# Attention kernel, two score phases: the 128-column round of heads 2, 3 ahead of the 64-column round

## The chip, the cores and the metric

The kernel runs on one core of a Trainium2 chip. The metric is device time in microseconds (us) for one launch, the median of several runs. TensorE (PE) does the matrix products, ScalarE (ACT) the exponentials and copies out of PSUM, VectorE (DVE) the additions, GpSimd (POOL) the causal masks, and SyncE (SP) issues most of the DMAs.

## The reference, cut to what matters

```python
B, C, H, W = x.shape                       # 32, 256, 32, 32; S = H * W = 1024
xf = group_norm(x).reshape(B, C, S)        # 32 groups
q = einsum('oc,bcs->bos', q_w, xf) + q_b   # 256 channels = 8 heads of 32
k, v = split(einsum('oc,bcs->bos', kv_w, xf) + kv_b)
scores = einsum('bhqd,bhkd->bhqk', q, k) / sqrt(32)
scores = where(mask == 0, -10000, scores)  # a key counts only if it is before the query
attn = where(mask == 0, 0, softmax(scores))
out = x + einsum('bhqk,bhkd->bhqd', attn, v)
```

Everything is float32. The trace shows each float32 matrix product of the program as two MATMUL rows, called its first and second pass below.

## The kernel before

The batch of 32 images is walked one after the other. The eight heads are two groups of four (`g` = 0, 1); head `j` of a group has rows 32j to 32j+31 of `q` and `k`, and so its own 32 rows of the PE array. Scores are made transposed: keys on partitions, queries along the free axis. Each group has six visits (`VISITS`), so an image has twelve, `v` = 0 to 11 (`v` = 6g + i). One visit consists of a score phase (`scores`, all of its products go through line 329), some projections (`pp`, `ppv`, line 173) and the products with the values of the visit before (`acc`, line 451). The whole order is written out by hand and kept as written; PE gets its instructions in this order.

A score phase fills three PSUM tiles of two banks. `pairs[0]` holds the long product of heads 0, 1, `pairs[1]` that of heads 2, 3, and `pairs[2]` (`short`) the short products of all four heads. In visits with a diagonal (`PAIRS`, i = 0, 1, 3, 4), `pair` builds the short product out of two rounds for each head: a 128-column round and a 64-column round. Each round is 2 heads x 2 halves of 64 keys, four products, which use four separate pieces of 32 rows x 64 columns of the array. So heads 2, 3 use one half of the array's rows and heads 0, 1 the other half, and products of the one half run beside products of the other.

The order in a phase: short rounds of heads 2, 3 (`first`); long product of heads 0, 1 (`begin`); long product of heads 2, 3; a wait of PE on the semaphore `bank_free`; short rounds of heads 0, 1. The wait is there because heads 0 and 2 share a bank of `short`, as do heads 1 and 3: the last product of each head and half of `first` (`made[-1]`) counts `bank_free` up. After the phase ACT takes the exponentials: of `pairs[0]`, of `pairs[1]`, and of `short`.

Some phases put a piece of the long product between the two rounds of heads 2, 3 (`between` in `scores_of`). In visit i = 0 this is a separate product of 128 columns. In the visits `v` = 3 and 4 (`SPLIT`; not in the last image) `part_of` makes two pieces of the long product of heads 0, 1: columns 0 to 127 and columns 128 to 511. `order` gives the sequence of the rounds: -1 turns it around, so that the 64-column round comes first. The visits `v` = 1, 7, 9 and 10 are not split: both rounds of heads 2, 3 follow each other, 128 columns first, and then comes the 512-column product of heads 0, 1.

Of the kernel before, what the change touches and what calls it, by code (L numbers as in the profile page):

```python
# [32 lines left out]
def tile_norm_attention_residual(  # L33
# [69 lines left out]
    def unshifted():  # L103
# [230 lines left out]
        def scores_of(b, g, bank_of, heads, entries, between=lambda: None, order=slice(None)):  # L334

            done = {}
            for _, _, halves in entries:
                for k, n in enumerate(list(range(max(map(len, halves))))[order]):
                    if k:
                        between()  # L340
                    for j in heads:
                        for c, ops in enumerate(halves):
                            if n < len(ops):
                                done.setdefault((j, c), []).append(score(b, g, bank_of(j), j, ops[n]))
            return done

        def part_of(b, g, bank, entry, of):

            at, _, halves = entry
            for j in (0, 1):  # L350
                for ((c, kb, first, _, cols),) in halves:
                    score(b, g, bank[:, j, :], j, (
                        c, kb, first + of.start, of.stop - of.start, slice(cols.start + of.start, cols.start + of.stop)
                    ))

        def mask(b, g, raw, j):


            hf, place = j // 2, (2 * j % 4) * P
            if ("e", b, g, "D", hf) not in live:  # L360
                live["e", b, g, "D", hf] = epool.tile(
                    [P, 4, HALF], F32, tag=("e0", "e")[hf], bufs=4, name=f"diagonal_{b}_{g}_{hf}"
                )
            square = live["e", b, g, "D", hf]
            for s in range(2):
                nc.gpsimd.affine_select(  # L366
                    out=square[:, :, place + s * P : place + (s + 1) * P],
                    in_=raw[:, :, (1 - s) * KEYS : (3 - s) * KEYS],
                    pattern=[[0, 4], [(1, -1)[s], P]], compare_op=ALU.is_gt, fill=0.0, base=0,
                    channel_multiplier=(-1, 1)[s],  # L370
                )
            if j == 0:
                nc.gpsimd.memset(square[0:1, :, 0:1], 1.0)

        def scores(b, v):


            g, i = divmod(v, len(VISITS))
            longs, shorts = VISITS[i]
            name = f"{b}_{g}_{i}"  # L380
            e = epool.tile([P, 4, HALF], F32, tag="e0" if i == TOTAL else "e", bufs=4, name=f"e_{name}")
            eh = epool.tile([P, 4, HALFBANK], F32, tag="eh", bufs=3, name=f"eh_{name}")
            pairs = [ps_s.tile([P, 2, HALF], F32, tag="sT", name=f"sT_{name}_{a}") for a in range(3)]
            short = pairs[2].rearrange("p bank (n q) -> p bank n q", n=2)
            short_of = lambda heads, *how: scores_of(
                b, g, lambda j: short[:, j % 2, j // 2, :], heads, shorts, *how
            )
            long_of = lambda heads, n: scores_of(b, g, lambda j: pairs[j // 2][:, j % 2, :], heads, longs[n : n + 1])
            rest = [lambda: long_of((2, 3), 1)] if len(longs) > 1 else []
            begin = [lambda n=n: long_of((0, 1), n) for n in range(len(longs) - 1, -1, -1)]  # L390
            if b < B - 1 and v in SPLIT:
                begin = [lambda n=n: part_of(b, g, pairs[0], longs[0], n) for n in (slice(0, P), slice(P, HALF))]
            if i in PAIRS and len(begin) > 1:
                first = short_of((2, 3), begin.pop(0), slice(None, None, -1))
            else:
                first = short_of((2, 3))
            for f in begin:
                f()
            long_of((2, 3), 0)

            ends = [made[-1] for made in first.values()]
            first = [ins for made in first.values() for ins in made]
            for ins in ends:
                ins.then_inc(bank_free, 1)
            for ins in first:
                tc.no_tile_sem_insts.add(ins.ins.name)
            live["free"] = live.get("free", 0) + len(ends)
            wait = nc.tensor.wait_ge(bank_free, live["free"])
            for ins in first:
                tc.declare_no_dep(wait.ins, ins.ins, reason="the semaphore orders them")  # L410
            made = short_of((0, 1), *rest if i in PAIRS else ())
            if i not in PAIRS:
                for f in rest:
                    f()
            for made in made.values():
                for lo in made:
                    for ins in first:
                        tc.declare_no_dep(lo.ins, ins.ins, reason="the semaphore orders them")
            wide, narrow = (max(at + width for at, width, _ in entries) for entries in (longs, shorts))
            for a in range(3):  # L420
                if a == 2:
                    exp = nc.scalar.activation(  # L422
                        eh.rearrange("p (n bank) q -> p bank n q", n=2)[:, :, :, :narrow], short[:, :, :, :narrow], AF.Exp
                    )
                else:
                    nc.scalar.activation(e[:, 2 * a : 2 * a + 2, :wide], pairs[a][:, :, :wide], AF.Exp)  # L426

            for ins in first:
                tc.add_to_no_dep_group(f"first_{name}", ins.ins)
                tc.add_to_no_dep_group("first", ins.ins)  # L430
            tc.declare_no_dep(exp.ins, group=f"first_{name}", reason="through the last two products")
            tc.declare_fence(exp.ins, group=f"first_{name}")
            live["e", b, g, "L", i], live["e", b, g, "H", i] = e, eh
            if i in PAIRS:
                mask(b, g, eh, PAIRS[i])
# [255 lines left out]
        with tc.manual_schedule(engines={ENG.PE, ENG.Activation, ENG.DVE, ENG.Pool, ENG.SP}):  # L691
# [47 lines left out]
            for b in range(B):  # L739
                first, last = b * N, b == B - 1  # L740
# [44 lines left out]
            for i in range(B * N + 1):  # L785
                if i < B * N:
                    scores(*divmod(i, N))
                for f in at.pop(i, ()):
                    f()
                b, v = divmod(i - 1, N)  # L790
                if i == B * N:

                    sums(3, SUMMED[v], False)
                if i:
                    for _ in range(EVEN.count((i - 1) % N) if i < B * N - N else 0):
                        nc.tensor.wait_ge(bank_free, live["free"])
                    values(b, v)
                    if b < B - 1 or v not in SUMMED or v == 1:
                        add_keys(b, v)
                if i in (B * N - 2, B * N - 1):  # L800

                    sums(3, SUMMED[v])
                for f in after.pop(i, ()):
                    f()
# [175 lines left out]
```

## Time and profile before

| | before |
|---|---|
| runs, median (lowest to highest) | 1791.58 us (1791.32 to 1792.56), 3 runs |
| profiled execution, span from first to last instruction | 1791.2 us |
| PE busy | 1782.1 us (99%) |
| DVE busy | 1669.4 us (93%) |
| ACT busy | 1441.4 us (80%) |
| POOL busy | 897.9 us (50%) |
| mean granted PE clock | 0.999 |
| one score phase `v` = 3, to the start of the next work on PE | 1.39 us |

The profiled execution is one run more, beside the three timed ones; its page gives the span and no further time. It is 0.4 us under the median and 0.1 us under the lowest run. Of the span, 31% of the chain of work that ended last is in the score products of line 329, all phases together. In the profile's rows `sT` stands for any of the three PSUM tiles of scores, and a form such as "32*64 32x128" is a product with 32 rows and 64 columns of weights and 128 moving columns. The end of a MATMUL row is modelled; its start is recorded.

### The profile page before, as it was taken

How to read it: one execution, taken by the hardware profiler on the slowest of the kernel's cores; microseconds unless marked ns; L12 is line 12 of the kernel's file. 1: busy time of each engine (PE TensorE's matmuls, PEld its weight loads, DVE VectorE, ACT ScalarE, POOL GpSimd, SP SyncE). 2: the span in 40 equal slices, each digit the busy share in tenths (PEclk: the TensorE clock that was granted, in tenths of full speed). 3: DMA queues.
4: the chain of work that ended last, by engine and by line, in shares of the span. 5: the costliest groups of instructions: out<-in, count | busy, mean ns of one | idle time of the engine just before them, and what ended most of it. 6: DMA issues, size and time to landing. Idle time of an engine off the chain costs nothing.

```text
span 1791.2 us, 81784 instructions
## 1 busy us (share of the span) xinstructions
PE 1782.1 (99%) x37036; PEld 936.1 (52%) x37036; DVE 1669.4 (93%) x1796; ACT 1441.4 (80%) x1928; POOL 897.9 (50%) x935
## 2 busy tenths in 40 slices
PE   9999999999999999999999999999999999999998
PEld 5555555555555555555555555555555555555554
DVE  4689999999999999999999999999999999999998
ACT  6888878888778788788887888877888878888785
POOL 2355554554555555545555555454455554554542
PEclk9999999999999999999999999999999999999999
DMA  2567766767677676676776676767766766777663
GB/s 72 105 117 142 137 133 135 148 138 147 128 142 138 137 141 138 132 144 142 142 138 134 137 142 138 150 129 140 139 145 131 141 136 135 149 138 141 133 109 98
DMA packets 92771, 240.21 MB, mean 134 GB/s; under 512 B 26272, under 2 KB 27792, under 8 KB 76544
## 3 DMA queue, kind: packets, MB, share of 16 engines
q0 software_dynamic: 17360, 100.58, 40.1%
q1 hardware_dynamic: 74912, 134.28, 25.9%
q8 instruction: 290, 4.75, 1.1%
q14 instruction: 65, 0.53, 0.1%
q10 hardware_dynamic: 144, 0.07, 0.0%
HBM read 69.90 MB, written 34.95 MB: 59 GB/s over the span
## 4 chain that ended last, share of the span: by engine, by line
PE 99%; DVE 0%; ACT 0%; issue 0%; POOL 0%; POOLq 0%
PE sT L329 31%; PE acc L451 28%; PE pp L173 27%; PE ppv L173 13%; PE pd L503 1%; PE busy L159 0%; PE wt L152 0%; ACT e L426 0%; DVE rb_last L576 0%; DVE rb_last L563 0%; DVE turned L560 0%; DVE acc L573 0%; DVE inv_last L562 0%; POOL ident masks.py:199 0%; PE pv L173 0%
## 5 line engine op out<-in xcount | busy, mean ns | idle before, releaser
L426 ACT ACTIVATE e<-sT 128x1024 f32<-128x1024 f32 x768 | 744.3, 1022 | 301.5 <-PE sT L329 298.8
L366 POOL TENSOR_SCALAR_AFFINE_SELECT diagonal<-eh 128x512 f32<-128x512 f32 x512 | 563.3, 1122 | 625.4 <-ACT eh L422 624.7
L469 DVE TENSOR_TENSOR e<-e,e 128x1024 f32<-128x1024 f32 x314 | 578.0, 1841 | 23.0 <-ACT v L293 3.5
L329 PE MATMUL sT<-q,k 32*64 32x64 f32 (+1 forms) x18928 | 577.9, 367 | 0.1
L329 PEld LDWEIGHTS sT<-q,k 32*64 32x64 f32 x18928 | 397.0, 131 | 203.8 <-PE sT L329 67.4
L173 PE MATMUL pp<-xn,wT 128*32 128x512 f32 x4096 | 492.3, 598 | 0.0
L451 PE MATMUL acc<-e,v 128*32 128x512 f32 (+3 forms) x4608 | 401.0, 450 | 0.0
L422 ACT ACTIVATE eh<-sT 128x768 f32<-128x768 f32 (+1 forms) x384 | 341.6, 890 | 0.0
L451 PEld LDWEIGHTS acc<-e,v 128*32 128x32 f32 x4608 | 149.2, 110 | 261.5 <-issue 239.0
L173 PE MATMUL ppv<-wT,xn 128*32 128x256 f32 x4096 | 247.5, 382 | 0.0
L469 DVE TENSOR_TENSOR diagonal<-diagonal,e 128x1536 f32<-128x1536 f32 x126 | 194.5, 1544 | 16.1 <-PE acc L451 6.5
L173 PEld LDWEIGHTS pp<-xn,wT 128*32 128x32 f32 x4096 | 107.0, 109 | 195.8 <-issue 163.7
L469 DVE TENSOR_TENSOR e<-e,eh 128x1024 f32<-128x1024 f32 x126 | 177.6, 1410 | 6.5
L451 PEld LDWEIGHTS acc<-diagonal,v 128*32 128x32 f32 x4096 | 120.9, 110 | 88.1 <-issue 68.2
L173 PEld LDWEIGHTS ppv<-wT,xn 128*32 128x32 f32 x4096 | 120.2, 109 | 80.0 <-issue 7.0
L469 DVE TENSOR_TENSOR e<-e,diagonal 128x2048 f32<-128x2048 f32 x63 | 144.0, 2285 | 18.9 <-POOL diagonal L366 18.7
L451 PE MATMUL acc<-diagonal,v 128*32 128x128 f32 x4096 | 158.9, 273 | 0.0
L205 POOL DMA_INDIRECT eight<-each,group_of x31 | 42.9, 1383 | 193.4 <-DMA each<-st 193.4
L262 ACT ACTIVATE xn<-x,shift,rstd 128x256 f32<-128x256 f32 x248 | 137.2, 614 | 0.8 <-POOL shift L247 0.8
L576 DVE SCALAR_TENSOR_TENSOR rb<-num,v_bias_col,x 128x256 f32<-128x256 f32 x248 | 121.5, 530 | 4.4
L482 POOL DMA_DIRECT2D e<-e x124 | 103.6, 835 | 42.6 <-issue 42.6
L482 POOL DMA_DIRECT2D diagonal<-diagonal x124 | 105.1, 847 | 0.7
(87 smaller groups left out, 1092.2 us busy)
## 6 DMA issues: line engine op xcount, KB each, us to landing
x<-in_x_dram SPq DMA_DIRECT2D x124, 256.0 KB, 3.8
diagonal<-diagonal POOLq DMA_DIRECT2D x62, 512.0 KB, 6.1
e<-e POOLq DMA_DIRECT2D x62, 512.0 KB, 5.7
rb<-inverses SPq DMA_DIRECT2D x124, 256.0 KB, 4.0
out_dram<-rb SPq DMA_DIRECT2D x124, 256.0 KB, 4.2
diagonal<-diagonal POOLq DMA_DIRECT2D x62, 256.0 KB, 4.6
folded<-diagonal SPq DMA_DIRECT2D x62, 256.0 KB, 5.1
e<-e POOLq DMA_DIRECT2D x62, 256.0 KB, 4.6
```

The source lines that it names most:

```text
L173: nc.tensor.matmul(out[part], lhsT=lhsT[:, part], rhs=rhs, start=start, stop=stop, skip_group_check=True)
L205: nc.gpsimd.indirect_dma_start(eight, None, live["each", b].rearrange("(m c) s -> m (c s)", c=CPG), bass.IndirectOffsetOnAxis(ap=group_of[ ...
L262: nc.scalar.activation(to, of, AF.Identity, bias=live["shift", b][:, g : g + 1], scale=rstd)
L329: return nc.tensor.matmul(bank[c : c + KEYS, cols], lhsT=live["k", b, g][rows, kb * P + c : kb * P + c + KEYS], rhs=live["q", b, g][rows, ...
L366: nc.gpsimd.affine_select(out=square[:, :, place + s * P : place + (s + 1) * P], in_=raw[:, :, (1 - s) * KEYS : (3 - s) * KEYS], pattern=[ ...
L422: exp = nc.scalar.activation(eh.rearrange("p (n bank) q -> p bank n q", n=2)[:, :, :, :narrow], short[:, :, :, :narrow], AF.Exp)
L426: nc.scalar.activation(e[:, 2 * a : 2 * a + 2, :wide], pairs[a][:, :, :wide], AF.Exp)
L451: nc.tensor.matmul(acc[HD * j : HD * (j + 1), of], lhsT=live["v", b][:, kb, h * HD : (h + 1) * HD], rhs=e[:, j, :], start=first, stop=last ...
L469: nc.vector.tensor_add(to, to, tile_of(b, g, at))
L482: nc.gpsimd.dma_start(out=total[:rows], in_=total[rows : 2 * rows], accum_op=ALU.add)
L503: nc.tensor.matmul(pd[HD * j : HD * (j + 1), of], lhsT=pick, rhs=e[:, j, :], start=start, stop=stop, skip_group_check=True,)
L576: nc.vector.scalar_tensor_tensor(blocks(rb, s), blocks(num, s, (start + s) % 2 == 1), v_bias_col[:, g : g + 1], blocks(xt[:, g, cols], s), ...
```

## The change

In a phase whose long product is one entry (`len(longs)` = 1) and which has a piece between the rounds, the rounds of heads 2, 3 are no longer turned around. This holds for `v` = 3 and 4 of the first 31 images, 62 phases. Visit i = 0 has two long entries and keeps its order.

```diff
             if i in PAIRS and len(begin) > 1:
-                first = short_of((2, 3), begin.pop(0), slice(None, None, -1))
+                first = short_of((2, 3), begin.pop(0), slice(None, None, -1 if len(longs) > 1 else 1))
             else:
                 first = short_of((2, 3))
```

PE's list at the start of the phase `v` = 3 of the first image, as a difference. In the names, `sT_0_3_0` is `pairs[0]` of group 0, visit 3, and `sT_0_3_2` is `short`; a form 64x128 is 64 output partitions x 128 columns.

```order
 L451 MATMUL acc_0_0_464<-diagonal_0_0_376,v_306 32x128 x8
+L329 MATMUL sT_0_3_2_547<-q_0_284,k_0_295 64x128 x4
+L329 MATMUL sT_0_3_0_545<-q_0_284,k_0_295 64x128 x4
 L329 MATMUL sT_0_3_2_547<-q_0_284,k_0_295 64x64 x4
-L329 MATMUL sT_0_3_0_545<-q_0_284,k_0_295 64x128 x4
-L329 MATMUL sT_0_3_2_547<-q_0_284,k_0_295 64x128 x4
 L329 MATMUL sT_0_3_0_545<-q_0_284,k_0_295 64x384 x4
 L329 MATMUL sT_0_3_1_546<-q_0_284,k_0_295 64x512 x4
```

The two rounds of heads 2, 3 have changed places; the 128-column piece of heads 0, 1 stays second, and the 384-column piece fourth.

PE's list with its waits in the phase `v` = 4 of the first image, from the first round to the last: first before, then now.

```order
L329 MATMUL sT_0_4_2_624<-q_0_284,k_0_295 64x64 [waits Activation_49]
L329 MATMUL sT_0_4_2_624<-q_0_284,k_0_295 64x64 x3
L329 MATMUL sT_0_4_0_622<-q_0_284,k_0_295 64x128 [waits Activation_49]
L329 MATMUL sT_0_4_0_622<-q_0_284,k_0_295 64x128 x3
L329 MATMUL sT_0_4_2_624<-q_0_284,k_0_295 64x128 x4
L329 MATMUL sT_0_4_0_622<-q_0_284,k_0_295 64x384 x4
L329 MATMUL sT_0_4_1_623<-q_0_284,k_0_295 64x512 [waits Activation_49]
L329 MATMUL sT_0_4_1_623<-q_0_284,k_0_295 64x512 x3
L329 MATMUL sT_0_4_2_624<-q_0_284,k_0_295 64x128 [waits bank_free]
```

The same place in PE's list with the change:

```order
L329 MATMUL sT_0_4_2_624<-q_0_284,k_0_295 64x128 [waits Activation_49]
L329 MATMUL sT_0_4_2_624<-q_0_284,k_0_295 64x128 x3
L329 MATMUL sT_0_4_0_622<-q_0_284,k_0_295 64x128 [waits Activation_49]
L329 MATMUL sT_0_4_0_622<-q_0_284,k_0_295 64x128 x3
L329 MATMUL sT_0_4_2_624<-q_0_284,k_0_295 64x64 x4
L329 MATMUL sT_0_4_0_622<-q_0_284,k_0_295 64x384 x4
L329 MATMUL sT_0_4_1_623<-q_0_284,k_0_295 64x512 [waits Activation_49]
L329 MATMUL sT_0_4_1_623<-q_0_284,k_0_295 64x512 x3
L329 MATMUL sT_0_4_2_624<-q_0_284,k_0_295 64x128 [waits bank_free]
```

The waits stand at the same places. What counts `bank_free` up is now the 64-column round, third in the phase, where it was the 128-column round in the same place. The lists of DVE, ACT, POOL and SP are the same row for row.

## The prediction

> **What bounds the kernel.** The page comes first: busy time, clock and the chain of work that ended last.
>
> ```profile
> PE 1782.1 (99%) x37036; PEld 936.1 (52%) x37036; DVE 1669.4 (93%) x1796; ACT 1441.4 (80%) x1928; POOL 897.9 (50%) x935
> PEclk9999999999999999999999999999999999999999
> PE 99%; DVE 0%; ACT 0%; issue 0%; POOL 0%; POOLq 0%
> ```
>
> PE is the chain almost alone and its clock is granted throughout, so a nanosecond of PE's order in these phases is a nanosecond of the kernel; a nanosecond of another engine is not, as long as PE does not come to wait for it. Next the timeline of PE, for the two phases that change (v = 3 and 4, early and late in the run), for two that are like them but not split (v = 9 and 10), and for v = 5, whose first round has 256 columns; then three rows in which full-height products of 512 columns follow each other. Columns: start, duration to the last modelled end, engine, line, first form, count.
>
> ```profile
> 141.77 1.46 PE L329 MATMUL sT<-q,k 32*64 32x64 f32 x56
> 143.16 1.93 PE L173 MATMUL ppv<-wT,xn 128*32 128x256 f32 x32
> 151.29 1.55 PE L329 MATMUL sT<-q,k 32*64 32x256 f32 x48
> 152.77 1.92 PE L173 MATMUL pp<-xn,wT 128*32 128x512 f32 x16
> 169.25 1.47 PE L329 MATMUL sT<-q,k 32*64 32x128 f32 x48
> 170.65 1.93 PE L173 MATMUL ppv<-wT,xn 128*32 128x256 f32 x32
> 1682.28 1.46 PE L329 MATMUL sT<-q,k 32*64 32x64 f32 x56
> 1683.66 1.93 PE L173 MATMUL ppv<-wT,xn 128*32 128x256 f32 x32
> ...
> 121.54 1.04 PE L173 MATMUL pp<-xn,wT 128*32 128x512 f32 x8
> 122.40 1.04 PE L451 MATMUL acc<-e,v 128*32 128x512 f32 x8
> 123.26 0.62 PE L451 MATMUL acc<-diagonal,v 128*32 128x128 f32 x16
> ```
>
> Three readings. A split phase takes 1.39 us from its start to that of the next work on PE (141.77 to 143.16; 1.38 at 1682.28), a phase without the split 1.40 (169.25 to 170.65): split and turned order together are worth some 0.01 us a phase. In all of these the next work starts 0.07 us before the phase's last modelled end (1.46 - 1.39, 1.47 - 1.40, 1.55 - 1.48): the phase's last row sets when PE goes on. And eight rows of 512 columns, two passes of four side by side, take 0.86 us (121.54 to 122.40, 122.40 to 123.26), so a pass of 512 columns takes 0.43 us, 0.84 ns a column.
>
> **The two halves of the array.** By that pace, heads 2, 3 have 64 + 128 + 512 columns in two passes, 1408 x 0.84 ns = 1.18 us; heads 0, 1 have 128 + 384 + 128 + 64, again 1408 columns and 1.18 us. The change alters neither sum. It reorders heads 2, 3 alone, and their first 192 columns only: 64 then 128 becomes 128 then 64. So it can cost or bring time in three ways: heads 0, 1 start one of their pieces at another time, heads 2, 3 start their 512 columns at another time, or the wait on bank_free ends later.
>
> **Heads 0, 1.** Their first piece has 128 columns; their second has 384, so its rows can be told from all others. The groups by form (count, busy, mean ns), for PE, from the start of the split phase at 141.772 to 0.028, to 0.288 and to 0.318 us behind it:
>
> ```profile
> L329 PE MATMUL sT<-q,k 32*64 32x128 f32 x1 | 0.3, 318 | 0.0
> ...
> L329 PE MATMUL sT<-q,k 32*64 32x128 f32 x14 | 0.5, 283 | 0.0
> L329 PE MATMUL sT<-q,k 32*64 32x64 f32 x8 | 0.3, 241 | 0.0
> ...
> L329 PE MATMUL sT<-q,k 32*64 32x384 f32 x4 | 0.5, 481 | 0.0
> ```
>
> The first 128-column row starts at about 0.03 us, behind the four of the 64-column round; the four first passes of 384 columns start between 0.288 and 0.318 us. Two passes of 128 columns are 0.21 us, so there is a hole of 0.05 us (0.29 - 0.03 - 0.21). Phase v = 5 shows the same for a first round that is not short: 256 columns of heads 2, 3, then 128 of heads 0, 1, then 384 of heads 0, 1. The same view from 151.29 to 0.29 and to 0.33 us behind it:
>
> ```profile
> L329 PE MATMUL sT<-q,k 32*64 32x256 f32 x8 | 0.7, 400 | 0.0
> L329 PE MATMUL sT<-q,k 32*64 32x128 f32 x8 | 0.4, 293 | 0.0
> ...
> L329 PE MATMUL sT<-q,k 32*64 32x384 f32 x4 | 0.5, 481 | 0.0
> ```
>
> Again all four start between 0.29 and 0.33. With 64 columns ahead and with 256, heads 0, 1 keep the same time; 128 lies between. I take 0 for this term. The far bound is the unsplit phase, +0.01 to 0.02 us a phase (1.40 against 1.39 and 1.38; 62 x 0.015 = 0.9 us), if the first piece came as late behind the rounds as there; against it stands that the 128-column piece keeps its second place in PE's list. Below nothing: a piece can't start earlier than second.
>
> What of the 64-column round, now ahead of the 384 columns in the list? In the unsplit phase v = 9 it stands ahead of 512 columns of heads 0, 1. The same view, 169.246 to 169.40:
>
> ```profile
> L329 PE MATMUL sT<-q,k 32*64 32x512 f32 x4 | 0.7, 638 | 0.0
> L329 PE MATMUL sT<-q,k 32*64 32x128 f32 x4 | 0.3, 318 | 0.0
> ```
>
> At 0.15 us the 512 columns run, and no row of the 64-column round has started, though it comes earlier in the list: rows of one half of the array don't wait for earlier products of the other half that are still queued. So the 384 columns need not wait for the 64-column round.
>
> [...]
>
> **Heads 2, 3.** Which half ends last, and by how much? The rows of line 329 that still run in the windows 143.221 to 143.224 and 143.225 to 143.229, at the end of the split phase (count, then shortest, median and longest duration, starts, forms):
>
> ```profile
> L329 PE MATMUL sT<-q,k x2: 217/402/587, 142.6 to 143.0; 32*64 32x512 f32 x1, 32*64 32x64 f32 x1
> L329 PE MATMUL sT<-q,k x1: 587/587/587, 142.6 to 142.6; 32*64 32x512 f32 x1
> ```
>
> The last row is one of heads 2, 3's 512 columns, and heads 0, 1's last 64 columns end between 1 and 8 ns before it, about 5. In the unsplit phase it is the other way (170.67 to 170.72):
>
> ```profile
> L329 PE MATMUL sT<-q,k x4: 217/217/217, 170.5 to 170.5; 32*64 32x64 f32 x4
> ```
>
> There the 512 columns are through and four 64-column rows remain. The reason shows in their starts. Line 329's rows on PE (the x) 0.803 to 0.813 us behind the start of each phase, and again just behind the fourth start, of v = 3 (142.575, 142.645) and v = 9 (170.05, 170.085):
>
> ```profile
> 142.57:142.59 0.01, 0.01 (x8) 1.00 3.93 819
> 142.65:142.66 0.01, 0.01 (x12) 1.00 0.00 0
> 170.05:170.06 0.01, 0.01 (x8) 1.00 13.76 1638
> 170.09:170.09 0.01, 0.01 (x12) 1.00 0.00 0
> ```
>
> Four second passes of 512 columns join the eight rows in both phases, but in v = 9 all within 0.035 us, in v = 3 over up to 0.07. In v = 9 heads 2, 3 run 128, then 64, then 512: the order that the change gives to v = 3 and 4. So the 512 columns should end some 0.03 us earlier, and heads 0, 1's 64 columns, 5 ns earlier than today's last row, become the last. The phase gets 5 ns shorter (bounds 0 and 8, by the two windows): 62 x 5 ns = 0.3 us, between 0 and 0.5.
>
> **The wait.** It stands ahead of the last short rounds, on PE itself: all of PE's work queues behind it. The weights of heads 0, 1's first 128-column round load only when it ends. Line 329's rows on PE and PEld (weight loads) in two windows of 0.13 us on either side of that, in v = 3 (from 0.588 and from 0.728 us behind its start) and in v = 9 (from 0.574 and from 0.734), where the round that counts bank_free up last is the 64-column one, as the change makes it in v = 3 and 4:
>
> ```profile
> 142.36:142.49 0.13, 0.13 (x12) 0.00 (x0) 1.00 0.41 63
> 142.50:142.63 0.13, 0.13 (x15) 0.13 (x4) 1.00 2.98 504
> ...
> 169.82:169.96 0.14, 0.14 (x12) 0.00 (x0) 1.00 1.05 132
> 169.98:170.12 0.14, 0.14 (x12) 0.14 (x4) 1.00 0.98 117
> ```
>
> In both, no weights load up to 0.71, and four do from 0.73 on. These rounds' rows of the array come free when the 384 columns are through, at 0.29 + 2 x 0.32 = 0.93 us, so the wait has about 0.2 us to spare, with the 64-column round last as well. Price 0; the far bound is that it ends later by the 0.06 us that heads 2, 3's first round gets longer, which the 0.2 cover.
>
> **The sum.** Heads 0, 1: 0. The exit: -0.3 us. The wait: 0. DVE, ACT, POOL and SP keep their lists; ACT's second exponential gets its scores up to 0.03 us earlier and goes on waiting or working as before, off the chain. The profiled execution would go from a span of 1791.2 to 1790.9; it stands 0.4 us under the median, so the median goes from 1791.58 to about 1791.3 us. A difference under 0.2%, 3.6 us, or 58 ns a phase, can't be told from no change here; this forecast is a tenth of that.
>
> **The rivals.** (1) Slower, by program order: the 384 columns start only when the 64-column round's second pass has started or ended. In the new order this round follows two passes of 128 columns, 0.21 us, and the hole of 0.05 that heads 0, 1 show above, so its second pass starts at 0.32 and, four rows after each other, ends at 0.38 to 0.40. That is 0.03 to 0.10 us behind 0.29, all of it on heads 0, 1 and thus on the chain: 62 x 0.03 to 0.10 = 1.9 to 6.2 us, 1793.5 to 1797.8. It counts as slower from 58 ns a phase on, that is if the second pass must end. For it: in today's split phase the 384 columns start just as the second passes of the 128-column round do, so that phase can't refute it. Against it: v = 9, above. (2) The split is undone in effect: heads 0, 1 come as late as in the unsplit phase; 62 x 0.015 = +0.9 us, 1792.5. (3) The change doesn't reach the end: the 512 columns still start one after the other over 0.07 us, since their weights are still loaded beside other loads, and the phase stays at 1.39; 1791.6. (4) Faster beyond 0.2%: it would take 58 ns a phase, but heads 0, 1's sum alone, from the second place in the list, leaves 5 to 8; I know of no mechanism.
>
> **Chances and range.** Exit as worked out or unchanged, 1791.0 to 1791.6: 0.85 (rival 3 holds 0.25 of it). Rival 2: 0.08. Rival 1: 0.05, of which 0.02 passes the bound. Rival 4: 0.01; some effect not seen here, 0.01 slower. So faster 0.01, same 0.96, slower 0.03. The range adds what the runs themselves scatter (1791.32 to 1792.56, 1.2 us, with lucky and unlucky medians on both sides) and rival 2: 1790.3 to 1792.9.
>
> **What would show it.** In the changed trace: split phases 1.38 us from start to start; 384 columns starting between 0.29 and 0.32 as now; the four second passes of 512 columns starting together near 0.81 to 0.84; a 64-column row as the phase's last; the weight loads behind the wait still at 0.73. A first pass of 384 columns behind 0.33 would mean program order; a phase of 1.40 would mean rival 2.

## The result: slower by 0.4%

| | before | with the change |
|---|---|---|
| runs, median (lowest to highest) | 1791.72 us (1791.32 to 1792.56), 5 runs | 1798.57 us (1797.73 to 1800.65), 5 runs |
| ratio | | 1.004, 95% interval 1.0027 to 1.0052 |
| profiled execution, span | 1791.2 us | 1796.1 us |
| phase `v` = 3, start to start of the next work on PE | 1.39 us | 1.49 us |
| phase `v` = 9, not touched | 1.40 us | 1.40 us |

The forecast was 1791.3 us and no difference that can be told; the kernel is 6.9 us slower. The page after, beside the one in the prediction, shows no other bound: PE is still the chain.

```profile
PE 1786.2 (99%) x37036; PEld 941.7 (52%) x37036; DVE 1675.5 (93%) x1796; ACT 1441.5 (80%) x1928; POOL 891.0 (50%) x935
PE 99%; DVE 0%; DMA 0%; issue 0%; ACT 0%; SPq 0%
```

The timeline of PE after, for the changed phases `v` = 3 and 4 and the untouched `v` = 9:

```profile
141.94 1.56 PE L329 MATMUL sT<-q,k 32*64 32x128 f32 x56
143.43 1.93 PE L173 MATMUL ppv<-wT,xn 128*32 128x256 f32 x32
147.01 1.56 PE L329 MATMUL sT<-q,k 32*64 32x128 f32 x56
148.50 1.93 PE L173 MATMUL ppv<-wT,xn 128*32 128x256 f32 x32
...
169.62 1.47 PE L329 MATMUL sT<-q,k 32*64 32x128 f32 x48
171.02 1.06 PE L173 MATMUL ppv<-wT,xn 128*32 128x256 f32 x14
```

A changed phase takes 1.49 us (141.94 to 143.43, 147.01 to 148.50) instead of 1.39, the untouched one 1.40 as before. By the recorded starts it is 1491 against 1387 ns, the same in all 62 phases to 3 ns: 62 x 0.104 = 6.4 us, nearly all of the 6.9. The two profiled spans lie only 4.9 us apart: the profile of before holds two pauses of PE, of 0.2 and 0.9 us, that the profile after does not, and 0.4 us more ahead of the first and behind the start of the last score phase. Most of the longer pause lies in a visit with a first round of 256 columns; its phase, 1.55 us long at 151.29, is 2.25 long there:

```profile
618.82 2.25 PE L329 MATMUL sT<-q,k 32*64 32x256 f32 x48
```

Where a run lists both, the launch takes 1.7 us more than the span, 1797.83 against 1796.1 us for the profiled one after. So the profiled execution of before took about 1792.9 us, an estimate, and lies above its median; its span must not be set beside times of launches.

Where in the phase? The last rows of line 329 still running 1.458 to 1.475 us behind the start of the changed phase (count; shortest, median, longest duration; first and last start; forms):

```profile
L329 PE MATMUL sT<-q,k x3: 587/587/588, 142.9 to 142.9; 32*64 32x512 f32 x3
```

Three second passes of heads 2, 3's 512 columns end last, and they started at 142.9, 0.94 us or more behind the start; in the prediction's window of before all four had started by 0.88. The same view shows when the first passes of the 512 columns start, 0.450 to 0.460, 0.465 to 0.468 and 0.50 to 0.51 us behind the start:

```profile
L329 PE MATMUL sT<-q,k x17: 214/267/590, 142.1 to 142.3; 32*64 32x64 f32 x8, 32*64 32x128 f32 x4, 32*64 32x384 f32 x4, 32*64 32x512 f32 x1
L329 PE MATMUL sT<-q,k x16: 214/243/636, 142.1 to 142.4; 32*64 32x64 f32 x8, 32*64 32x384 f32 x4, 32*64 32x128 f32 x2, 32*64 32x512 f32 x2
L329 PE MATMUL sT<-q,k x13: 214/481/637, 142.2 to 142.4; 32*64 32x64 f32 x5, 32*64 32x384 f32 x4, 32*64 32x512 f32 x4
```

One of the four starts on time (0.384 by its recorded start); the other three start at 0.463, 0.479 and 0.496, where before they started at 0.392, 0.399 and 0.406: 0.07 to 0.09 us late. Their weights load 0.004 us ahead of their start, those of the first one 0.056 ahead (0.328 to 0.384), and their second passes follow 0.48 us behind the first instead of its 0.43. Of the 64-column rows ahead of them in their half the last starts at 0.346, and 64 columns at 0.84 ns take 0.05 us, so their piece of the array should be idle from about 0.40 on, an estimate. Before, the last of them needed 0.464 (0.406 to 0.870), now 0.478 (0.496 to 0.974): 0.090 us of later start and 0.014 of longer way are the 0.104 of the phase. The 384-column rows of heads 0, 1 are all running, on time.

### The profile page after: what moved, and what is told of

It reads as the page before. It is cut to its first block, busy times and chain, and to the rows that moved or that the text cites. A ratio compares the mean times of both kernels' runs of the same rounds, so it can differ in the third digit from the quotient of the medians.

```text
span 1796.1 us, 81784 instructions
## 1 busy us (share of the span) xinstructions
PE 1786.2 (99%) x37036; PEld 941.7 (52%) x37036; DVE 1675.5 (93%) x1796; ACT 1441.5 (80%) x1928; POOL 891.0 (50%) x935
## 3 DMA queue, kind: packets, MB, share of 16 engines
q8 instruction: 290, 4.75, 1.1%
## 4 chain that ended last, share of the span: by engine, by line
PE 99%; DVE 0%; DMA 0%; issue 0%; ACT 0%; SPq 0%
PE sT L329 30%; PE acc L451 28%; PE pp L173 26%; PE ppv L173 14%; PE pd L503 1%; DMA x<-in_x_dram 0%; DVE st L189 0%; PE wt L152 0%; ACT e L426 0%; DVE rb_last L576 0%; DVE rb_last L563 0%; PE busy L159 0%; DVE turned L560 0%; DVE acc L573 0%; DVE inv_last L562 0%
## 5 line engine op out<-in xcount | busy, mean ns | idle before, releaser
L366 POOL TENSOR_SCALAR_AFFINE_SELECT diagonal<-eh 128x512 f32<-128x512 f32 x512 | 556.9, 1108 | 639.9 <-ACT eh L422 636.4
L329 PEld LDWEIGHTS sT<-q,k 32*64 32x64 f32 x18928 | 403.2, 131 | 196.8 <-PE sT L329 57.7
```

The costliest lines, as they stand in the source:

```text
L329: return nc.tensor.matmul(bank[c : c + KEYS, cols], lhsT=live["k", b, g][rows, kb * P + c : kb * P + c + KEYS], rhs=live["q", b, g][rows, ...
L366: nc.gpsimd.affine_select(out=square[:, :, place + s * P : place + (s + 1) * P], in_=raw[:, :, (1 - s) * KEYS : (3 - s) * KEYS], pattern=[ ...
```

## What holds the three products back

The order of products in the phase gives a count: rounds of four, heads 2, 3 (products 1 to 4), heads 0, 1 (5 to 8), heads 2, 3 (9 to 12), heads 0, 1 (13 to 16), and then the 512 columns (17 to 20). The three late ones are 18 to 20; the 17th, the first of the 512s, is on time. When does the first product end? Rows of 128 columns after, in the windows 0.421 to 0.426 and 0.430 to 0.433:

```profile
L329 PE MATMUL sT<-q,k 32*64 32x128 f32 x8 | 0.3, 268 | 0.0
...
L329 PE MATMUL sT<-q,k 32*64 32x128 f32 x7 | 0.3, 268 | 0.0
```

The first one's second pass ends (by the model) at 0.428, and the 18th starts 0.035 us behind it. Before, the first is a 64-column product; rows of 64 columns at 0.318 to 0.322 and 0.326 to 0.329, and then line 329's weight loads running at 0.340 to 0.352 and 0.357 to 0.367:

```profile
L329 PE MATMUL sT<-q,k 32*64 32x64 f32 x4 | 0.2, 217 | 0.0
...
L329 PE MATMUL sT<-q,k 32*64 32x64 f32 x3 | 0.2, 217 | 0.0
```

```profile
142.11:142.12 0.01, 0.01 (x5) 1.00 0.00 0
142.13:142.14 0.01, 0.01 (x6) 1.00 0.00 0
```

It ends at 0.324, and one more weight load, the 18th product's, starts between 0.352 and 0.357, by its record 0.355. So both orders fit one count, the window theory below: PE takes a product of its list in only when the one 17 places ahead of it has ended. This is the author's reading of these times; what in PE holds the product back no trace shows. The 18th comes in 0.031 us behind the end of the first, and the next ones every 0.017 us. The change made the first product end later, at 0.428 instead of 0.324, and so moved the window. Before, the weights of the three products loaded at 0.355 to 0.388, just in time for first passes that start at 0.386 to 0.406; now they load at 0.459 to 0.492, for first passes at 0.463 to 0.496.

## The experiments

The first four ran once each, on a chip where the kernel before took 1795.93 us (one run, 2 to 5 us over its medians elsewhere). Single runs scatter by some us (11 of before on another chip took 1790.79 to 1796.27), so the totals don't add up from the phases, and the phases, the same in nearly all images, are what is compared. The theories, besides the window: collision (weight loads of heads 0, 1 at the same time as those of the 512-column products of heads 2, 3, "the 512s", hold these back) and half (a 512 behind a 64-column round in the same half of the array comes late in a phase cut in two).

**Another cut.** Changed order, first piece 384 columns, second 128.

```diff
-                begin = [lambda n=n: part_of(b, g, pairs[0], longs[0], n) for n in (slice(0, P), slice(P, HALF))]
+                begin = [lambda n=n: part_of(b, g, pairs[0], longs[0], n) for n in (slice(0, 3 * P), slice(3 * P, HALF))]
```

> The changed order, but the long product of heads 0, 1 is cut into 384 + 128 columns instead of 128 + 384. Window theory (PE's list takes a product in only when the product 17 places ahead of it has ended, then one every 0.017 us): the cut is no matter, the 18th product still waits for the end of the first, a 128-column one. The 512-column products of heads 2, 3 start at 0.38 (first) and 0.46 to 0.50 us (the other three), the phase takes 1.49 us, the kernel about 1798.5. Collision theory (the weights of the 512 columns are late because heads 0, 1 load weights for their second piece at 0.30 to 0.32 us, beside them): that load is now later than 0.4, the four 512s start together at 0.38, phase 1.38, kernel 1791.3. Half theory (512 columns behind a 64-column round in the same half come late by themselves in a phase cut in two): as with the window, 1.49 and 1798.5.

Measured: 1806.36 us, a phase of 1.62. Rows of line 329 at 0.43 to 0.44 and 0.50 to 0.51 us:

```profile
L329 PE MATMUL sT<-q,k x20: 214/268/590, 142.1 to 142.5; 32*64 32x384 f32 x8, 32*64 32x64 f32 x8, 32*64 32x128 f32 x3, 32*64 32x512 f32 x1
L329 PE MATMUL sT<-q,k x17: 214/481/637, 142.1 to 142.6; 32*64 32x384 f32 x8, 32*64 32x64 f32 x5, 32*64 32x512 f32 x4
```

The three products are late as with the change (0.463 to 0.496), though heads 0, 1 load the first weights of their second piece only at 0.402, when the 18th product is already late: collision falls. But no theory expected 1.62. The cause is the wait on `bank_free`. PE and PEld rows of line 329, first with the change at 0.69 to 0.73 and 0.746 to 0.876, then in this run at 0.91 to 1.12 and 1.135 to 1.25:

```profile
142.63:142.67 0.04, 0.04 (x12) 0.00 (x0) 1.00 0.00 0
142.68:142.81 0.13, 0.13 (x13) 0.13 (x4) 1.00 3.01 504
...
142.97:143.18 0.21, 0.21 (x16) 0.00 (x0) 1.00 0.33 117
143.19:143.31 0.12, 0.12 (x8) 0.12 (x8) 1.00 0.38 143
```

The weights behind the wait load at 1.132 instead of 0.744, though the round that counts the semaphore up ends no later (0.562 and 0.563, modelled). Ahead of this round in the list stands the 384-column piece, whose modelled end is 0.90.

**The 512s earlier in the list.** Changed order, 512 columns ahead of the 384.

```diff
-            for f in begin:
-                f()
-            long_of((2, 3), 0)
+            last = [lambda: long_of((2, 3), 0)]
+            for f in last + begin if b < B - 1 and v in SPLIT else begin + last:
+                f()
```

> The changed order, but the 512 columns of heads 2, 3 are written ahead of the 384 columns of heads 0, 1 (rounds of four: 128, 128, 64, 512, 384). Window: the 512s are now products 13 to 16 and start together at 0.384; the 384s are 17 to 20, the first at 0.30 and the other three at 0.46 to 0.50, with the second passes behind that; heads 0, 1 have more behind them, so the phase goes to about 1.60 us and the kernel to about 1805 (62 x 0.21 us over before). Half theory: the 512s still come behind the 64-column round and are as late as with the change, the 384s on time, phase 1.49, 1798.5. Collision: neither late, 1.38, 1791.3.

Measured: 1806.97 us, a phase of 1.61. Rows at 0.42 to 0.43 and 0.50 to 0.51:

```profile
L329 PE MATMUL sT<-q,k x21: 214/267/590, 142.4 to 142.7; 32*64 32x128 f32 x8, 32*64 32x64 f32 x8, 32*64 32x512 f32 x4, 32*64 32x384 f32 x1
L329 PE MATMUL sT<-q,k x13: 214/529/590, 142.6 to 142.8; 32*64 32x64 f32 x5, 32*64 32x384 f32 x4, 32*64 32x512 f32 x4
```

Now the four 512s are on time and three of the 384s are late, at 0.464 to 0.497, as the window has it: in this phase the place in the list decides, not the width or the half. Half falls. One detail missed: the 17th product started at 0.346, not at 0.30; its weights loaded at 0.294.

**More products ahead.** The kernel before, three pieces.

```diff
-                begin = [lambda n=n: part_of(b, g, pairs[0], longs[0], n) for n in (slice(0, P), slice(P, HALF))]
+                begin = [lambda n=n: part_of(b, g, pairs[0], longs[0], n) for n in (slice(0, P), slice(P, 2 * P), slice(2 * P, HALF))]
```

> The kernel before (64-column round first) with the long product of heads 0, 1 in three pieces, 128 + 128 + 256, so that 20 products stand ahead of the 512s instead of 16; the columns of each half are the same as before. Window: the 21st product waits only for the 4th (0.344 us) and the three before it at one every 0.017, so its weights load at about 0.405; the 22nd waits for the 5th, a 128-column product of heads 0, 1 that ends at 0.455, so 0.486, then 0.503 and 0.519. The phase goes from 1.39 to about 1.52 us, the kernel to about 1799.9. Half and collision theories: heads 2, 3 run in the order of before, 1.39, 1791.7.

Measured: 1805.64 us, a phase of 1.52 (in most images; six of the 31 phases `v` = 4 are longer). Rows at 0.42 to 0.43, 0.492 to 0.500 and 0.53 to 0.54:

```profile
L329 PE MATMUL sT<-q,k x21: 267/268/636, 142.6 to 142.9; 32*64 32x128 f32 x20, 32*64 32x512 f32 x1
L329 PE MATMUL sT<-q,k x14: 267/268/636, 142.7 to 142.9; 32*64 32x128 f32 x12, 32*64 32x512 f32 x2
L329 PE MATMUL sT<-q,k x20: 267/268/636, 142.7 to 143.0; 32*64 32x128 f32 x12, 32*64 32x512 f32 x4, 32*64 32x256 f32 x4
```

The weights loaded at 0.406, 0.486, 0.503 and 0.519 against 0.405, 0.486, 0.503 and 0.519 expected, from the ends of the 4th and 5th products. Here heads 2, 3 keep the order of before, and the phase is 0.13 us longer all the same.

**The long product whole between the rounds.** Twelve products ahead of the 512s.

```diff
-                begin = [lambda n=n: part_of(b, g, pairs[0], longs[0], n) for n in (slice(0, P), slice(P, HALF))]
-            if i in PAIRS and len(begin) > 1:
+                begin = [lambda: long_of((0, 1), 0)]
+            if b < B - 1 and v in SPLIT:
+                first = short_of((2, 3), begin.pop(0))
+            elif i in PAIRS and len(begin) > 1:
```

> The changed order of rounds, but the long product of heads 0, 1 stays whole between the two rounds (rounds of four: 128, 512, 64, 512): 12 products ahead of the 512s of heads 2, 3. Window: they start together at 0.384. But the last 64-column round of heads 0, 1 are products 21 to 24, and 22 to 24 now wait for products 5 to 7, the 512s of heads 0, 1, which end at 1.095: weights at 1.13 to 1.16, and the phase ends at 1.42 like that of visit 0, where the same holds. 62 x 0.03 = 1.9 us over before, 1793.6. Half theory: 512s behind 64s still late, 1.49, 1798.5. Collision theory: nothing loads beside the 512s' weights and nothing holds the last round, 1.38, 1791.3.

Measured: 1829.51 us, a phase of 1.86. Rows at 0.42 to 0.43, then PE and PEld at 1.13 to 1.36 and 1.375 to 1.50:

```profile
L329 PE MATMUL sT<-q,k x20: 214/268/638, 144.9 to 145.3; 32*64 32x512 f32 x8, 32*64 32x64 f32 x8, 32*64 32x128 f32 x4
```

```profile
146.04:146.28 0.23, 0.23 (x4) 0.00 (x0) 1.00 0.38 143
146.29:146.41 0.12, 0.12 (x8) 0.12 (x8) 1.00 1.46 393
```

The 512s of heads 2, 3 are on time with the others (eight at 0.42), as the window says and half does not. The total was missed by all: the weights behind the wait load at 1.370, while the counting 64-column round is the same as with the change. It stands in the list behind four 512-column products of heads 0, 1, whose modelled end is 1.11. Both misses, here and in the cut at 384 columns, fit one reading: a product can start before an earlier one of the other half (in `v` = 9 of before 512 columns of heads 0, 1 start at 0.053 us, the earlier 64-column round at 0.269), but its semaphore counts up only when those ahead of it have ended (loads behind the wait 0.23 and 0.26 us behind the modelled ends at 0.90 and 1.11). The next run tests this with a number:

**Cut in the middle.** Changed order, 256 + 256, on one chip with the next two.

```diff
-                begin = [lambda n=n: part_of(b, g, pairs[0], longs[0], n) for n in (slice(0, P), slice(P, HALF))]
+                begin = [lambda n=n: part_of(b, g, pairs[0], longs[0], n) for n in (slice(0, 2 * P), slice(2 * P, HALF))]
```

> The changed order with the long product of heads 0, 1 cut into 256 + 256. Window theory with ends in program order (a product counts its semaphore up only when all products ahead of it in the list have ended): the 18th product's weights still load at 0.459; the wait on bank_free now ends behind heads 0, 1's first piece, whose last second pass has its modelled end at about 0.69, so that the weights behind it load at about 0.90 (0.744 with the change, 1.13 with 384 columns first, 1.37 with all 512 first), just in time; phase 1.49 to 1.50. If products end in any order, the wait ends as with the change, at 0.744. Phase 1.49 either way; kernel 62 x 0.104 = 6.4 to 7 us over before.

Measured: 1798.87 us, a phase of 1.49, the 18th product's weights in the same place; PE and PEld at 0.70 to 0.90 and 0.92 to 1.04:

```profile
142.33:142.53 0.20, 0.20 (x13) 0.00 (x0) 1.00 1.97 328
142.55:142.67 0.12, 0.12 (x16) 0.12 (x8) 1.00 0.33 68
```

The wait ends with loads at 0.918, against 0.90 expected and 0.744 for ends in any order. The traces also record the counts themselves: one semaphore is counted up four times in each score phase, as `bank_free` is. In us behind the start of `v` = 3, ends modelled:

| columns of heads 0, 1 ahead of the counting round | these end | counting round ends | first and fourth count | weights behind the wait |
|---|---|---|---|---|
| 128 (with the change) | 0.475 | 0.563 | 0.575, 0.703 | 0.744 |
| 256 | 0.688 | 0.562 | 0.749, 0.876 | 0.918 |
| 384 | 0.901 | 0.562 | 0.962, 1.090 | 1.132 |
| 512 | 1.113 | 0.562 | 1.201, 1.328 | 1.370 |

The weights follow the fourth count by 0.041 to 0.042 us in each, and the counts follow the longer piece ahead. So at these three widths the counts come in program order, 0.061 to 0.088 us behind the modelled end of the piece ahead; whether the short products themselves end as late is not shown, since their ends are modelled.

**The change again, on the same chip.** 

> The change itself, beside the two others on one chip. Every theory here: phases of 1.49 us and 62 x 0.104 = 6.4 us over before, a ratio of 1.0036.

Measured: 1798.44 us against 1791.40 before (11 runs), ratio 1.0036 (1.0023 to 1.0049); phases of 1.49.

**The better version that was looked for.** The kernel before, the 64-column round first, split in all phases that allow it.

```diff
-        SPLIT = 3, 4
+        SPLIT = 1, 3, 4, 7, 9, 10
```

> The kernel before with its 64-column round first and the split in the visits 1, 7, 9 and 10 as well, so in all phases with one long product and a diagonal of the first 31 images. Window theory: a split phase with the 64-column round first takes 1.39 us, one without the split 1.40 (1387 and 1403 ns by the recorded starts), since the 18th product waits only for a 64-column one; 4 x 31 x 16 ns = 2.0 us less than before, a ratio of 0.9989. Half theory (a 512 behind a split is late when a 64-column round is just ahead of it): the same, since here 128 columns stand ahead of it. Rival for this run: the split does not carry over to visits with other neighbours, ratio 1.000 or above.

Measured: 1801.25 us, ratio 1.0047 (1.0035 to 1.0059), slower. The phases are as expected, 1387 ns in all six visits in most images, and an image without a pause takes 54.91 us against 54.98. But 15 visits of the image loop have pauses of 0.07 to 1.4 us, some 10 us together, in which PE waits for nothing that the profile shows; before has two, of 0.2 and 0.9. One of them in the timeline:

```profile
1181.87 1.46 PE L329 MATMUL sT<-q,k 32*64 32x64 f32 x41
1183.95 0.56 PE L329 MATMUL sT<-q,k 32*64 32x128 f32 x15 [0.62 <-issue]
```

The extra pieces add 64 rows of weight loads and products to PE's list in an image. The packets of the instruction queue went from 290 to 298 (before; all six split):

```profile
q8 instruction: 290, 4.75, 1.1%
```

```profile
q8 instruction: 298, 4.88, 1.2%
```

4.75 MB in 290 packets is 16 KB each. PE and PEld have 74,072 rows together, 255 to a packet, and the 1,984 rows more in this run went with 8 packets more, 248 rows each; so these packets look like PE's own instructions, some 250 rows each, an estimate from these counts. 64 rows are a quarter of one, and the pauses in visit 1 came at images 5, 9, 13, 17 and 21.

```diff
-        SPLIT = 3, 4
+        SPLIT = 3, 4, 9, 10
```

> The kernel before with the split in the visits 9 and 10 as well (four phases in each of 31 images instead of two). By the phases alone: 62 x 16 ns = 1.0 us less, ratio 0.9994. Fetch theory of the pauses in the run with all six phases split (PE's instructions come in packets of 16 KB, 256 of the rows of weight loads and products; 64 more rows an image moved the packets' edge by a quarter of a packet an image, and pauses of 0.3 to 1.4 us came at every fourth image): 32 more rows an image move it by an eighth, so pauses at the same place come at every eighth image, in total between none and the 10 us of that run, ratio 0.999 to 1.005. If the pauses belong to the split of the visits 1 and 7, none are left and the ratio is 0.9994.

Measured: 1801.99 us against 1793.53 before (9 runs, another chip), ratio 1.0041 (1.0028 to 1.0055), with some 25 pauses of 0.06 to 1.2 us. They came in visits 1, 4, 7 and 10, so they don't belong to the split of visits 1 and 7; but they did not come every eighth image, so the expected period missed. That the pauses are PE running out of instructions is argued from the counts, not shown. No version faster than the kernel before was found.

## Why the prediction was wrong, by its steps

- **PE's order in these phases is the kernel's time**: right. 62 x 0.104 = 6.4 us, of 6.9 measured.
- **Heads 0, 1: 0.** Right: their 384 columns start at 0.296 to 0.316 as before, ahead of the second passes of the 64-column round (0.325 on), which stands earlier in the list. So rival 1 did not happen.
- **Heads 2, 3: -0.3 us.** This step failed. It took the order 128, 64, 512 from `v` = 9 and expected the 512s to start together. But in `v` = 9 only 12 products stand ahead of the 512s; in a split phase 16 do, so that the second to fourth of the 512s are products 18 to 20 and by this count find the window full until the first product has ended (weights at 0.459 to 0.492, behind the modelled end at 0.428). The right reading was in the profile of before: the spread of the 512s' second passes over 0.07 us in `v` = 3 fits the same window (weights at 0.355, 0.372 and 0.388, behind the modelled end at 0.324). The prediction took it for loads that collide (rival 3), which the cut at 384 columns rules out. The term measured +0.104 us a phase instead of -0.005.
- **The wait: 0.** Right in size (loads at 0.744, needed by 0.94), in part by luck: the 0.2 us to spare were worked out from the counting round alone, and the piece of heads 0, 1 ahead of it, here only 128 columns, can use them up, as the later cuts show (loads at 1.132 and 1.370 behind 384 and 512 columns).
- **Rival 3** named the spread of the 512s and priced it at today's 0.07 us; nothing in it asked what sets the spread. No rival held the case that the runs fit, a window that the longer first product closes later.

What the window is in PE is not shown; it is argued from the count. When the held 18th product comes in, the 16 products behind the first stand ahead of it (with the change the weights of the 17th load at 0.328, before the first ends at 0.428, and those of the 18th at 0.459). Products of the two row halves don't start in program order (in `v` = 9 products of 512 columns start at 0.053, an earlier 64-column round at 0.269), while their counts come in it as far as the runs show (loads behind the wait at 0.918, 1.132 and 1.370).

## What to carry to other kernels

When products of two halves of the array run beside each other, count the products ahead of each one: here the weights of the 18th load 0.031 us behind the modelled end of the first, with three pieces those of the 22nd 0.031 behind that of the fifth, and a phase with 64 columns first is 0.104 us shorter than with 128. Compare with a similar phase only after counting: with 12 products ahead, as in `v` = 9, the four 512s start within 0.020 us (0.383 to 0.403), with 16 ahead and 128 columns first within 0.112 (0.384 to 0.496). And look at what stands ahead of a short product with a semaphore: here its count came 0.06 to 0.09 us behind the modelled end of a longer piece of the other half.

## What the runs showed of the hardware

- The 18th product's weights load 0.031 us behind the modelled end of the first (0.324 to 0.355, 0.428 to 0.459), the next ones 0.017 us apart; further down the list it holds alike (with three pieces, the 22nd at 0.486 behind the end of the fifth at 0.455). Why the weights of the 17th loaded only at 0.294 with the 512s earlier was not settled.
- The count of a 64-column round that stands behind a piece of 256, 384 or 512 columns of the other half comes 0.06 to 0.09 us behind the modelled end of that piece (0.749, 0.962 and 1.201 behind 0.688, 0.901 and 1.113), and four counts in a row come 0.043 us apart.
- With the change the three 512s whose weights load 0.004 us ahead of their start (0.459 to 0.492) need 0.05 us more before their second pass than the one whose weights load 0.056 ahead (0.48 instead of 0.43 us).
- Two or four more split phases an image shorten each by 16 ns and yet cost some 10 us in pauses in which PE waits for nothing visible; their cause stays open.
